# Graph attention with a planned order: five weight buffers in place of four, single buffers for the projections' pieces

## The chip, the core and the metric

The kernel runs on one core of a Trainium2 chip. A core has five engines with a queue each: TensorE (PE) multiplies matrices into PSUM, VectorE (DVE) and ScalarE (ACT) work elementwise on PSUM and SBUF, GpSimd (POOL) elementwise on SBUF, and SyncE (SP) issues transfers here. Each engine takes its instructions in the order of the program and waits on semaphores for what other engines owe it. The metric is the device time in microseconds (us) of one execution. Before the change three runs gave 6959.61 to 6975.31 us, with a median of 6971.53.

## What is computed

Two layers over a graph with N = 2708 nodes and D = 128 features. The second is small (two products of the 2708 x 2708 adjacency with a 2708 x 128 matrix). Nearly all the time is the attention of the first, which is unusual: after the projection, q, k and v are reshaped to (128, N, 8), so that there are 128 attentions, each over all N nodes with 8 channels, and all share one dense bias.

```python
q = (x @ Wq.T).reshape(d, n, h)          # d = 128, n = 2708, h = 8
k = (x @ Wk.T).reshape(d, n, h)
v = (x @ Wv.T).reshape(d, n, h)
a = jnp.einsum('dnh,dmh->dnm', q, k) * scale
a = a + adj + adj
a = jax.nn.softmax(a, axis=2)
out = jnp.einsum('dnm,dmh->dnh', a, v)
out = out.reshape(n, h * d) @ Wo.T
```

x is then normalised as layernorm(x + out), and the second layer follows. That makes 128 x 2708 x 2708, or 939 million, exponentials in float32.

## The kernel before

**Tiling.** The 128 attentions go in 32 groups of four (GB = 4), one per 32-row strip of TensorE. The queries of a group go in six blocks of 452 columns (QB; the last has 448). The 2708 keys are cut in 22 chunks: 21 of 128 and a short one of 20 (number NU = 21), whose four attentions share one tile. The scores lie transposed: keys on the partitions, queries along the row. The softmax takes no maximum away. The sum of the exps is had by a column of ones beside the values, so v has nine columns (VW).

**Steps and pieces.** The tiles (chunk, attention) of a block are shared out by `plan` over nine steps. A step has two to four *pieces* of two tiles each, 29 in a block, and one chunk called *two* of which three attentions' scores are taken another way. There are 32 x 6 x 9 = 1728 steps and 54 in a group. For a piece, TensorE writes two score tiles side by side into the PSUM tile s (`score`, L415, or L412 for the short chunk), and VectorE adds the adjacency to both and writes them into the step's tile e (`add_near`, L422). For the three tiles of *two*, TensorE writes scores into p, a PSUM tile with three banks. They are taken beside the pieces' own scores, on row strips that these leave free where possible. ScalarE takes the exp of p into w (L515) and GpSimd multiplies it by exp of twice the adjacency (L516, tile ecol), which stands for the addition. After a step's last piece ScalarE takes the exp of e in place (L518).

**Products.** When all four tiles of a chunk have their exps, `add_up` (L440; L437 for a block's first chunk, L432 for the short one) multiplies them with the values and adds into the single PSUM tile acc, one product per chunk, 22 in a block. A product of float32 shows as two instructions, so a chunk is eight of them. After a block's last product `hand_on` has VectorE copy acc to SBUF (L446) and SP store it in four transfers (L448).

**Buffers.** [...]s two tiles of two banks, p one of three, acc one. In SBUF, e has four buffers of 8 x 452 floats a partition (pool *weights*), w four (*products*), the adjacency comes in *cols* (9), *twos* (3) and *ecols* (7) and is issued eight tiles ahead by `load_adj`. The pool *proj* has two buffers each for four small tiles: xc (the chunk of x), wc (half of a weight matrix), pa (the projected half) and pr (that half rounded to the shorter float that the scores are multiplied in, and the remainder).

**Projections amid the attention.** Only two chunks of x are projected at the start. The rest, 120 halves, is projected in between, before piece 0 of the steps in `amid`: nine in group 0, six steps apart, then four in each group at its steps 2, 10, 18 and 26, until group 28. `project` has TensorE multiply wc into an s tile (L343), VectorE scale it into pa (L345), and leaves a list of *jobs*: for keys and queries two by GpSimd (L356, L357) and a store by SP (L352), for values the store alone (L347). One job is done per step, behind the score of its first piece (piece 1's position, L476). `load_half` for the next half is called at once, at the place of the projection.

**The order.** Nothing is left to a scheduler: instructions are issued as `interleave` yields them. It walks through a table of costs and decides whether TensorE goes on with a piece, a product or a projection. The argument `bufs` says how many e buffers it reckons with: a piece of step n is not to be had before the products with the tiles of step n - bufs stand in the order. It never yields a product before its exps are due by its costs. SP's queue follows the same program: the loads of a step at its piece 0, with eight transfers for the next block's queries at step 3 of a block (`load_q`, L287) ahead of that step's adjacency, and the stores of sums where `hand_on` comes.

Of the kernel before, what the change touches and what calls it, by code (L numbers as in the profile page):

```python
# [142 lines left out]
def graph_attention_gcn(ctx: ExitStack, tc: tile.TileContext, x, xT, adj, adjT, adjP, adjS,  # L143
# [20 lines left out]
    NU = NM - 1  # L164
# [24 lines left out]
    with ExitStack() as s:  # L189
# [28 lines left out]
        for m in range(NU):  # L218
            if m not in TWO_EXP:
                pairs += [[(m, 0), (m, 1)], [(m, 2), (m, 3)]]  # L220
            elif left_over.index(m) % 2:
# [4 lines left out]
        plan = [(pairs[cuts[i] : cuts[i + 1]], m, [j for j in range(GB) if j != left_out[m]])  # L226
                for i, m in enumerate(TWO_EXP)]
# [4 lines left out]
        steps = [(g, b, i) for g in range(NG) for b in range(len(QBS)) for i in range(len(plan))]  # L232
# [43 lines left out]
        def spread_values(g, j):  # L276
            to = vals[g % 2].rearrange("p c (j e) -> p j c e", e=VW)
            v = values[g][:, j, :].rearrange("p (c e) -> p c e", e=H)
            nc.gpsimd.tensor_copy(to[:, j, :, :H], v)
            nc.gpsimd.tensor_copy(v_first[g % 2][:, ds(32 * j, H)], v[:, first_chunk, :])  # L280

        def load_q(g, b):
            n0, nw = QBS[b]
            q = queries[g, b] = qpool.tile([P, QB], F32R, tag="q", name="q")
            for j in range(GB):
                for i in range(2):
                    nc.sync.dma_start(q[ds(32 * j + 2 * H * i, 2 * H), :nw].bitcast(F32),  # L287
                                      qs[:, ds((GB * g + j) * N + n0, nw)])
# [14 lines left out]
                nc.sync.dma_start(t[:, :nw], adjP[ds(m * P, P), ds(n0, nw)])  # L303

        ahead = 8
        epool = s.enter_context(tc.tile_pool(name="weights", bufs=4))
        ppool = s.enter_context(tc.tile_pool(name="products", bufs=4))
        opool = s.enter_context(tc.tile_pool(name="sums", bufs=2))
        proj = s.enter_context(tc.tile_pool(name="proj", bufs=2))
        ps = s.enter_context(tc.tile_pool(name="ps_s", bufs=2, space=PSUM))  # L310
        pq = s.enter_context(tc.tile_pool(name="ps_q", bufs=1, space=PSUM))
        pa = s.enter_context(tc.tile_pool(name="ps_a", bufs=1, space=PSUM))
# [15 lines left out]
        def load_half(n):  # L328
            c, i, h = halves[n]
            i0, mi = MC[c]  # L330
            if i == h == 0:
                given[c] = proj.tile([P, P], F32, tag="xc", name="xc")
                nc.sync.dma_start(given[c][:, :mi], xT[:, ds(i0, mi)])
            given[c, i, h] = proj.tile([P, NB], F32, tag="wc", name="wc")
            nc.sync.dma_start(given[c, i, h], projections[i][0][:, ts(h, NB)])

        def project(n):

            c, i, h = halves[n]
            i0, mi = MC[c]  # L340
            dst = projections[i][1]
            pp = ps.tile([P, 2, NB], F32, tag="s", name="s")
            nc.tensor.matmul(pp[:mi, 0, :], given[c][:, :mi], given.pop((c, i, h)), start=True, stop=True)  # L343
            a = proj.tile([P, NB], F32, tag="pa", name="pa")[:mi]
            nc.vector.tensor_scalar_mul(a, pp[:mi, 0], half_scale if i == 1 else 1.0)  # L345
            if i == 2:
                return [lambda: nc.sync.dma_start(dst.rearrange("(i g) e -> i (g e)", g=P)[ds(i0, mi), ts(h, NB)], a)]  # L347
            o = proj.tile([P, 2, NB], F32R, tag="pr", name="pr")[:mi]

            def store():  # L350
                for l in range(2):
                    nc.sync.dma_start(dst.rearrange("r (i g) -> i r g", g=P)[ds(i0, mi), ds(H * l + 4 * h, 4)],  # L352
                                      o[:, l].bitcast(F32).rearrange("p (e g) -> p e g", g=P))


            return [lambda: nc.gpsimd.tensor_copy(o[:, 0], a),  # L356
                    lambda: nc.gpsimd.tensor_sub(o[:, 1], a, o[:, 0].bitcast(F32)), store]  # L357
# [66 lines left out]
        def add_up(g, b, m, tiles):  # L424
            nw = QBS[b][1]
            _, _, v, vz = groups[g]
            if m == first_chunk:
                acc[g, b] = pa.tile([P, NB], F32, tag="acc", name="acc")
            a = acc[g, b]
            if m == NU:  # L430
                e, t = tiles[0]
                nc.tensor.matmul(a[:, :nw], vz, e[:, t, :nw], start=False, stop=False)  # L432
                return
            for j in range(GB):
                e, t = tiles[j]
                if m == first_chunk:
                    nc.tensor.matmul(a[ds(32 * j, 32), :nw], v_first[g % 2][:, ds(32 * j, 32)], e[:, t, :nw],  # L437
                                     start=True, stop=False)
                else:
                    nc.tensor.matmul(a[ds(32 * j, VW), :nw], v[:, m, ds(VW * j, VW)], e[:, t, :nw],  # L440
                                     start=False, stop=(m == last_chunk))

        def hand_on(g, b):
            n0, nw = QBS[b]
            o = opool.tile([P, QB], F32, tag="o", name="o")
            nc.vector.tensor_copy(o[:, :nw], acc.pop((g, b))[:, :nw])  # L446
            for j in range(GB):
                nc.sync.dma_start(os_[:, ds((GB * g + j) * N + n0, nw)], o[ds(32 * j, H + 1), :nw])  # L448
# [3 lines left out]
        amid = list(range(2, 54, 6)) + [54 * g + t for g in range(1, NG) for t in (2, 10, 18, 26)]  # L452
        amid = amid[: len(halves)]
        for g in range(1, NG):
            c = (min(NG, g + 2) * GB * N - 1) // (P * P)
            assert c < FIRST or amid[halves.index((c, 2, 1))] + 8 < 54 * g
        jobs = []
        loaded = ahead
        for what, n, c, beside in interleave(plan, len(steps) // len(plan), NU, amid):
            if what == "amid":  # L460
                at = amid.index(n)
                jobs += project(at)
                if at + 1 < len(halves):
                    load_half(at + 1)
                continue
            if what == "add_up":
                g, b = divmod(n, len(QBS))
                add_up(g, b, c, where.pop((g, b, c)))
                continue
            if what == "hand_on":  # L470
                hand_on(*divmod(n, len(QBS)))
                continue
            g, b, i = steps[n]
            pieces, two, _ = plan[i]
            nw = QBS[b][1]
            if c == 1 and jobs:  # L476
                jobs.pop(0)()
            if c == 0:
                nq = (g, b + 1) if b + 1 < len(QBS) else (g + 1, 0)
                if i == 3 and nq[0] < NG:  # L480
                    load_q(*nq)

                if g + 1 < NG:
                    t = b * len(plan) + i
                    if t < 32 and t % 2 == 0:
                        load_keys(g + 1, t // 2)
                    elif t < 32 and t % 8 == 7:
                        load_values(g + 1, t // 8)
                    elif 33 <= t < 50 and t % 2:
                        order_keys(g + 1, (t - 33) // 2)  # L490
                    elif t >= 50:
                        spread_values(g + 1, t - 50)
                last = max(loads.index((g, b, x), max(0, loaded - 40)) for x in [chunks_of(p) for p in pieces] + [-1 - two])
                while loaded < min(len(loads), last + 1 + ahead):
                    load_adj(loaded)
                    loaded += 1
                e = epool.tile([P, 8, QB], F32, tag="e", name="e")
                sp = pq.tile([P, 3, NB], F32, tag="p", name="p")
                w = ppool.tile([P, 3, QB], F32, tag="w", name="w")
                if g == 0:  # L500
                    first_exp(b, two)
                at = k = 0
            st = ps.tile([P, 2, NB], F32, tag="s", name="s")
            for r, (m, j) in enumerate(pieces[c]):
                score(st[:, r], g, b, m, j)
                where.setdefault((g, b, m), {})[j] = e, at + r
            for j in beside:
                score(sp[:, k], g, b, two, j)
                where.setdefault((g, b, two), {})[j] = w, k
                k += 1  # L510
            add_near(e, st, g, b, pieces[c], at)
            at += 2
            if c == len(pieces) - 1:
                look_at_near(g, b, two)
                nc.scalar.activation(w[:, :, :nw], sp[:, :, :nw], AF.Exp, scale=2.0)  # L515
                nc.gpsimd.tensor_mul(w[:, :, :nw], w[:, :, :nw],  # L516
                                     exp_cols[g, b, two][:, :nw].unsqueeze(1).to_broadcast([P, 3, nw]))
                nc.scalar.activation(e[:, :at, :nw], e[:, :at, :nw], AF.Exp, scale=2.0)  # L518
# [315 lines left out]
```

## Time and profile before

| | |
|---|---|
| timed runs, median (lowest to highest) | 6971.53 us (6959.61 to 6975.31) |
| profiled execution, its own time | 6986.59 us |
| its span | 6984.8 us |
| instructions in it | 137327 |
| mean TensorE clock granted, of full speed | 0.99 |
| moved by DMA | 1674.16 MB, mean 240 GB/s |
| first / last w exp (L515) starts at | 45.8 us / 6638.7 us |

The profile is one execution taken by the hardware. Busy time is the time in which an engine had an instruction running; matmuls are pipelined and their ends are modelled, so a busy TensorE is not one at its peak. "PEld" is its loading of weights, which lies beside the products. A group of instructions is told by its line in the kernel, engine, operation and tile. A wait is told by who waited (engine and line), who released it, the total of the idle time, how often and the longest. In the order of time, a line has the start and the duration in us, the engine, the line, the instruction, how many were merged into the line, and in brackets the idle time before it with what ended it. Stretches give, behind their length, the busy time of PE, PEld, DVE, ACT and POOL with the number of instructions, then the clock granted to TensorE, the share of DMA and GB/s.

The mean of one add on VectorE is 1091 ns, of one w exp 1340 ns, of one e exp 2677 ns (one for a whole step), of one multiply on GpSimd 3101 ns.

### The profile page before, as it was taken

The numbers are of one execution on the slowest core, as the hardware profiler recorded it, in microseconds if no ns is written. First come the engines' busy times: TensorE is split into PE (matmuls) and PEld (weight loads), VectorE is DVE, ScalarE is ACT, GpSimd is POOL, SyncE is SP. The second block draws the span as 40 slices with busy tenths as digits, with TensorE's granted clock in tenths as the row PEclk, the third lists the DMA queues.
The fourth block names the chain that finished last, engine by engine and source line by source line (L and its number), as shares of the span: only waits on it lengthen the run. The fifth ranks groups of instructions, "written<-read, shape, count | busy, mean of one in ns | idle before, by whom it ended". The sixth has DMA issues, their size and how long they took to land.

```text
span 6984.8 us, 137327 instructions
## 1 busy us (share of the span) xinstructions
PE 6734.9 (96%) x50426; PEld 2008.4 (29%) x50426; DVE 6129.9 (88%) x6307; ACT 6518.0 (93%) x3605; POOL 5761.0 (82%) x2546
## 2 busy tenths in 40 slices
PE   7999999999999999999999999999999999999979
PEld 2222222222222222222222222222222222222254
DVE  6899999999899999998998999999989999999941
ACT  7999999999999999999999999999999999999920
POOL 6888888888888888888888988889888888888800
PEclk8999999999999999999999999999999999999999
DMA  8877877777788777877777788877777877777667
GB/s 270 263 243 245 244 240 239 229 236 237 239 243 247 242 239 242 252 239 242 239 237 231 243 256 246 249 236 240 234 235 242 247 243 235 235 228 233 218 200 229
DMA packets 1143258, 1674.16 MB, mean 240 GB/s; under 512 B 148922, under 2 KB 1090366, under 8 KB 1138478
## 3 DMA queue, kind: packets, MB, share of 16 engines
q1 hardware_dynamic: 1142574, 1665.29, 77.5%
q8 instruction: 399, 6.54, 0.4%
q14 instruction: 285, 2.33, 0.1%
HBM read 1582.90 MB, written 81.80 MB: 238 GB/s over the span
## 4 chain that ended last, share of the span: by engine, by line
PE 48%; DMA 15%; DVE 12%; ACT 9%; issue 7%; SPq 5%; POOL 4%; DVEq 0%; ACTq 0%; POOLq 0%
PE acc L440 22%; PE s L415 16%; DVE e L422 10%; DMA col<-in_adjP 8%; ACT e L518 5%; POOL w L516 4%; ACT w L515 4%; PE acc L661 3%; DMA two<-in_adjP 2%; SPq L287 2%; PE acc L432 2%; PE p L415 2%; DMA ecol<-ne 2%; PE acc L437 1%; PE s L343 1%
## 5 line engine op out<-in xcount | busy, mean ns | idle before, releaser
L516 POOL TENSOR_TENSOR w<-w,ecol 128x1356 f32<-128x1356 f32 (+1 forms) x1728 | 5347.8, 3101 | 840.5 <-ACT w L515 740.9
L422 DVE TENSOR_TENSOR e<-s,col 128x904 f32<-128x904 f32 (+1 forms) x4608 | 4830.5, 1091 | 347.7 <-PE s L415 175.4
L518 ACT ACTIVATE e<-e 128x2712 f32<-128x2712 f32 (+5 forms) x1728 | 4625.7, 2677 | 33.5 <-DVE e L422 31.9
L440 PE MATMUL acc<-e,vals 128*9 128x452 f32 x20352 | 3591.7, 548 | 0.4 <-ACT e L518 0.2
L415 PE MATMUL s<-q,k 32*128 32x452 f32 x10944 | 2465.0, 465 | 175.3 <-DVE e L422 113.0
L515 ACT ACTIVATE w<-p 128x1356 f32<-128x1356 f32 (+1 forms) x1728 | 2316.0, 1340 | 98.7 <-PE p L415 84.1
L415 PEld LDWEIGHTS s<-q,k 32*128 32x128 f32 x10944 | 1016.3, 182 | 3414.6 <-DVE e L422 2974.0
L440 PE MATMUL acc<-w,vals 128*9 128x452 f32 x10368 | 1631.1, 547 | 0.0
L415 PE MATMUL p<-q,k 32*128 32x452 f32 (+1 forms) x5184 | 1334.6, 443 | 5.0 <-ACT w L515 4.4
L422 DVE TENSOR_TENSOR e<-s,two 128x904 f32<-128x904 f32 (+1 forms) x960 | 1047.8, 1091 | 173.7 <-PE s L415 92.9
L440 PEld LDWEIGHTS acc<-e,vals 128*9 128x9 f32 x20352 | 443.0, 88 | 782.1 <-issue 778.5
L415 PEld LDWEIGHTS p<-q,k 32*128 32x128 f32 x5184 | 546.1, 183 | 43.3 <-ACT w L515 29.5
L440 PEld LDWEIGHTS acc<-w,vals 128*9 128x9 f32 x10368 | 206.7, 88 | 221.9 <-issue 186.4
L262 POOL CAST k<-k_raw 128x336 fp32r<-128x336 f32 x251 | 222.3, 886 | 34.7 <-DMA q<-qs 34.7
L437 PE MATMUL acc<-e,v_first 128*32 128x452 f32 (+1 forms) x1536 | 187.5, 560 | 13.2 <-DVE o L446 3.6
L432 PE MATMUL acc<-e,v_short 128*128 128x452 f32 (+1 forms) x384 | 196.7, 594 | 0.0
L343 PE MATMUL s<-wc,xc 128*128 128x512 f32 (+1 forms) x240 | 133.8, 639 | 0.7 <-DVE e L422 0.4
L345 DVE TENSOR_SCALAR pa<-s 128x512 f32<-128x512 f32 (+1 forms) x120 | 82.8, 690 | 52.5 <-PE s L343 51.8
L446 DVE COPY o<-acc 128x452 f32<-128x452 f32 x192 | 118.4, 617 | 6.5 <-PE acc L440 6.5
L661 PE MATMUL acc<-col,xw 128*128 128x512 f32 (+2 forms) x264 | 106.0, 551 | 0.0
L661 PE MATMUL acc<-col,hw 128*128 128x512 f32 (+2 forms) x264 | 104.1, 545 | 0.0
L555 ACT ACTIVATE sd<-mv,eps 128x1 f32<-128x1 f32 (+1 forms) x22 | 5.9, 291 | 104.7 <-DVE mv L549 104.7
(84 smaller groups left out, 1067.2 us busy)
## 6 DMA issues: line engine op xcount, KB each, us to landing
col<-in_adjP SPq DMA_DIRECT2D x1965, 226.0 KB
two<-in_adjP SPq DMA_DIRECT2D x1440, 226.0 KB
ecol<-ne SPq DMA_DIRECT2D x1395, 226.0 KB
col<-in_adjP SPq DMA_DIRECT2D x393, 224.0 KB
two<-in_adjP SPq DMA_DIRECT2D x288, 224.0 KB
ecol<-ne SPq DMA_DIRECT2D x279, 224.0 KB
col<-in_adjT SPq DMA_DIRECT2D x210, 256.0 KB
k_raw<-ks SPq DMA_DIRECT2D x512, 84.6 KB
```

What stands on the lines that cost most here:

```text
L262: copy(k[:, :, ts(i, n)], t[:, ts(i, n * NU)].rearrange("p (q c) -> p c q", c=NU))
L287: nc.sync.dma_start(q[ds(32 * j + 2 * H * i, 2 * H), :nw].bitcast(F32), qs[:, ds((GB * g + j) * N + n0, nw)])
L343: nc.tensor.matmul(pp[:mi, 0, :], given[c][:, :mi], given.pop((c, i, h)), start=True, stop=True)
L415: nc.tensor.matmul(to[:, :nw], k[r, m, :], q[r], start=True, stop=True)
L422: nc.vector.tensor_add(e[:, ds(at, 2), :nw], st[:, :, :nw], a)
L432: nc.tensor.matmul(a[:, :nw], vz, e[:, t, :nw], start=False, stop=False)
L437: nc.tensor.matmul(a[ds(32 * j, 32), :nw], v_first[g % 2][:, ds(32 * j, 32)], e[:, t, :nw], start=True, stop=False)
L440: nc.tensor.matmul(a[ds(32 * j, VW), :nw], v[:, m, ds(VW * j, VW)], e[:, t, :nw], start=False, stop=(m == last_chunk))
L515: nc.scalar.activation(w[:, :, :nw], sp[:, :, :nw], AF.Exp, scale=2.0)
L516: nc.gpsimd.tensor_mul(w[:, :, :nw], w[:, :, :nw], exp_cols[g, b, two][:, :nw].unsqueeze(1).to_broadcast([P, 3, nw]))
L518: nc.scalar.activation(e[:, :at, :nw], e[:, :at, :nw], AF.Exp, scale=2.0)
L661: nc.tensor.matmul(acc[:, :nw], src[:mw, m, :], t[:mw, :nw], start=(m == 0), stop=(last is None and m == NM - 1))
```

## The change

The pool of e tiles gets a fifth buffer and `interleave` is called with `bufs=5`. The pool *proj* goes from two buffers to one for each of its four tiles. And the load of the next half is no longer issued at the projection: it becomes the last of the jobs, so it comes up three steps after the projection for keys and queries and one step after for values.

```diff
         ahead = 8
-        epool = s.enter_context(tc.tile_pool(name="weights", bufs=4))
+        epool = s.enter_context(tc.tile_pool(name="weights", bufs=5))
         ppool = s.enter_context(tc.tile_pool(name="products", bufs=4))
         opool = s.enter_context(tc.tile_pool(name="sums", bufs=2))
-        proj = s.enter_context(tc.tile_pool(name="proj", bufs=2))
+        proj = s.enter_context(tc.tile_pool(name="proj", bufs=1))
...
-        for what, n, c, beside in interleave(plan, len(steps) // len(plan), NU, amid):
+        for what, n, c, beside in interleave(plan, len(steps) // len(plan), NU, amid, bufs=5):
             if what == "amid":
                 at = amid.index(n)
                 jobs += project(at)
                 if at + 1 < len(halves):
-                    load_half(at + 1)
+                    jobs.append(lambda n=at + 1: load_half(n))
                 continue
```

An e tile takes 8 x 452 x 4 = 14464 bytes of a partition; the four tiles of *proj* together take 512 + 2048 + 2048 + 4096 = 8704 bytes, so the change adds 5760 bytes to a partition. The w tiles (*products*) stay at four and PSUM stays as it is.

Through `bufs`, the whole order of TensorE's instructions changes, and with it the place of `hand_on`: in the old order it comes behind piece 1 of a block's step 2 or just before the next, in the new order at step 3, which is behind the call of `load_q` in the program. The number of instructions of every kind stays the same.

## The prediction

> **What bounds the kernel now.** I read the shares of busy time first, then busy time by stretch, then the waits, then the order of instructions where a stretch loses time. Columns of a wait: total us, number of times, longest. One group is 54 steps; a step has one w exp and one e exp on ScalarE (L515, L518).
>
> ```profile
> PE 6734.9 (96%) x50426; PEld 2008.4 (29%) x50426; DVE 6129.9 (88%) x6307; ACT 6518.0 (93%) x3605; POOL 5761.0 (82%) x2546
> ```
>
> By share TensorE leads. By stretch it does not. These rows are busy times in three stretches cut at the start of a w exp: groups 8, 13 and 30.
>
> ```profile
> 1743.58:1954.33 210.75, 201.52 (x1542) 57.20 (x1538) 186.65 (x185) 201.66 (x109) 180.83 (x81) 0.98 0.78 237
> 2760.84:2963.55 202.71, 199.37 (x1542) 57.13 (x1538) 186.55 (x185) 200.91 (x110) 179.07 (x79) 1.00 0.81 245
> 6249.84:6450.00 200.16, 197.03 (x1533) 57.14 (x1531) 184.01 (x181) 200.16 (x109) 175.76 (x75) 1.00 0.75 233
> ```
>
> The fourth busy time is ScalarE's. In group 30, which has no projections, it is busy for 200.16 of 200.16 us: that is the floor of a group. Group 13, a quiet one with four projections, takes 202.71; group 8 takes 210.75, with the clock at 0.98. The starts of L515 in order of time give groups 1 to 28 together 5759.9 us; 28 floors of 200.2 are 5605.6. So **154 us** are lost where ScalarE starves, some 4 more in group 0, nothing after group 28. Who starves it:
>
> ```profile
> DVE e L422 <- PE s L415: 268.3, 654, 2.6
> ...
> ACT w L515 <- PE p L415: 84.1, 133, 3.3
> ```
>
> So TensorE is late for VectorE far more often than ScalarE stands still; only the second costs time. Two kinds of place carry the loss. The first is a projection, here group 13's at its step 18, seen on VectorE and then ScalarE (start, duration):
>
> ```profile
> 2826.26 0.69 DVE L345 TENSOR_SCALAR pa<-s 128x512 f32<-128x512 f32 x1 [0.42 <-PE s L343]
> ```
> ```profile
> 2831.36 3.22 ACT L518 ACTIVATE e<-e 128x3616 f32<-128x3616 f32 x1 [0.78 <-DVE e L422]
> ```
>
> VectorE idles 0.42 us for the projection's product, spends 0.69 on it, and five adds later ScalarE has nothing to exponentiate for 0.78 us. Such quiet groups (10, 13, 19, 22: 202.7 to 203.2) lose 2.6 us or so each: 28 x 2.6 = **73 us**. The rest, 154 - 73 = **81 us**, falls on groups of 204 to 211 us, mostly six steps into a block. Here is why, in SP's queue and on VectorE in group 8:
>
> ```profile
> 1813.74 2.44 SPq L448 DMA_DIRECT2D os<-o  x4
> 1816.47 5.45 SPq L287 DMA_DIRECT2D q<-qs  x8
> 1821.96 0.42 SPq L299 DMA_DIRECT2D ecol<-ne  x1
> 1822.43 0.43 SPq L296 DMA_DIRECT2D two<-in_adjS  x1
> ```
> ```profile
> 1827.90 1.10 DVE L422 TENSOR_TENSOR e<-s,two 128x904 f32<-128x904 f32 x1 [4.52 <-DMA two<-in_adjP]
> ```
> ```profile
> 1822.00:1832.00 10.00, 5.84 (x32) 1.56 (x27) 4.50 (x5) 7.60 (x5) 5.82 (x3) 0.72 0.92 263
> ```
>
> SP stores the sums and loads the next queries back to back, 8 us; the adjacency tile behind them lands 4.5 us late; TensorE idles, and its clock falls to 0.72 in those ten us.
>
> **The change, part by part.** *Order of products.* The order was worked out so that piece 0 of step n stands behind all products of step n-4; now n-5. Written out for both values, before 53% of the products stand three steps behind their last exp's step and the rest two steps; after, 31% stand four behind, 64% three. Between comparable pieces one or two products (0.88 us each, 2827.77 to 2828.65 in TensorE's timeline) move behind scores, so scores reach VectorE 0.9 to 1.8 us earlier after a projection. That is as much as a projection takes away (0.42 + 0.69). TensorE can pay it back, though barely: by its starts a block is 22 products of 0.88, 30 score pairs of 0.40 and six pairs of row groups met twice, 1.1 more, together 32.5 us; six blocks and four projections of 0.95 are 198.8, under ScalarE's 200.2. Against part one's 73 us: bounds 0 and 73. I take three quarters, **-55**, nearer the full one because the delays are about one product long; late next is the single p tile (the scores for the w exp wait until the last w exp has read it), which stays. A rule speaks against this: the Trainium skill, "TensorEngine Tiling", section PSUM Bottleneck, has tiling speed up TensorE but not the emptying of PSUM, which may become the bound; an SBUF buffer would then bring 0 and the sum stays 6985. The row says VectorE, which empties s, is busy 186.55 of 202.71 us, and it waits for TensorE 268 us in all; I follow the row.
>
> The new order also has 308 products directly behind another for 230, each 0.76 for 0.88 us (2833.74 to 2834.50 in the timeline): 78 x 0.12 = 9 us; and 939 pieces whose p scores share a row group for 1094, each 0.60 for 0.41 us (2831.61 to 2832.21 against 2827.36 to 2827.77): 155 x 0.19 = 29 us. Both lie beside ScalarE's work and are counted as nothing, but raise TensorE's room from 1.4 us a group to 2.6.
>
> *What else moves with it: hand-on.* The copy of the sums follows the last product, so it moves from piece 1 or 2 of a block's step 2 to piece 0 or 1 of step 3. Its four stores in SP's queue thereby pass behind the eight query loads and the adjacency loads issued at step 3 (three tiles, four DMAs). SP waits for that copy 983.2 us in all (176 times, up to 9.7); the query loads fill this wait instead of following it. At one such place late in the run SP issues nothing between 6240.31 and 6248.40, then four stores (1.39 us), eight queries (3.56 us) and only then a tile. After the change a tile follows the stores at once, 3.6 to 5.5 us earlier; the late tile was 4.5 us late. The skill's "DMA: Bandwidth & Descriptors", section Issuing engines are not separate DMA queues, holds the sequencer's time to issue for usually small beside the DMA; by it this move is worth 0. Here eight queries of 28.2 KB take 5.45 us to issue, and at the mean 240 GB/s their 226 KB take 0.94 us to move. The row decides: of 81 us, bounds 0 and 81, I take 60%, **-49**. The copy itself is between the same neighbours on VectorE and the first product of the next block still has two pieces before it: nothing.
>
> *Single buffers for projections.* xc, wc, pa and pr get one buffer; the load of the next half becomes a job, issued three steps after the projection (one for values) in place of with it, behind that step's adjacency and query loads, before the hand-on's stores where they meet. Each half adds one or two DMAs to another place in SP's queue (0.33 us each). Steps take 3.7 to 4.3 us and projections lie 6 or 8 steps apart, so the load has three steps left in group 0 and five later, 13 us and more. From DMAs issued and bytes moved I work out 3 to 4 us to landing. The product's buffer is free three steps before. pa is read by GpSimd's two copies (1.29 us for the second) two steps into the half, pr is stored by SP the step after, and both have three steps or more until rewritten. Bounds 0 and 120 halves x 1 us; I take **0**, hidden behind three or more steps of exps. Behind a late weight TensorE would hold scores, and with them all.
>
> *A new wait.* The w tiles remain four. The product that reads w of step n-4 now stands behind piece 0 of step n in 1136 steps, which costs nothing while it precedes the last piece; in 38 steps (mostly step 31 of a group) it stands behind it, and w's exp of step n waits for it. Behind that exp stand e's exp on ScalarE, GpSimd's multiply and the next p scores. A product is 0.88 us and about 0.2 until seen: 0 to 38 x 1.1 = 41 us. There ScalarE has little lead (0.2 us idle at step 31 in quiet groups), so I take a third, **+14**.
>
> Sum: -55 - 49 + 0 + 14 = -90. The profiled execution took 6986.6 (span 6984.8), so 6897; the three timed runs have a median of 6971.5, 15 below it, so **6880** as a median (6971.5 - 90, rounded).
>
> **Rivals.** *Full:* both losses go and ScalarE never starves before the end. For it: groups 29 to 31 run so with the same PSUM. Against it: clock drops. 6971.5 - 158 + 14 = 6828; 110 us or more gained is this case. *PSUM holds:* lead is set by one p and two s tiles, buffered products only wait elsewhere. For: TensorE waits for VectorE to free s (113 us). Against: 654 waits the other way. Only the queries' move pays, half of it: 6971.5 - 25 = 6946, down to no change. *Slower:* w is the bottleneck, four w tiles under an order for five. Place: L515 waiting for L440, in any of the 1136 steps where TensorE is late, ScalarE idling directly. Each wait costs up to a product and its signal, 1.1 us; from 104/1.1 = 95 waits, three or four a group, it decides; at six a group, 168 x 1.1 = 185, it gives 6971.5 - 104 + 185 = 7052. For: ScalarE is the bound. Against: the order has only 38 behind the last score. *It does not do what it says:* the order could hold nothing back because exps come late anyway; then 6971. Against: the products' places written out do shift.
>
> **How the numbers follow.** Forecast (40 to 110 gained) 0.52; full 0.20; PSUM or no effect 0.17, of which 0.10 gains more than 14 us; slower 0.11. A change within 0.2% (14 us) cannot be told from none. Faster 0.82, same 0.07, slower 0.11. The range leaves out the slower case and the outer part of full: 6830 to 6955.
>
> **What would show it.** Right: idle of L515 for p below 40 us; VectorE's idle for two and col (29.6 and 13.7) near a third; SP's wait for o well under 983; clock near 1.00 six steps into blocks; groups with projections at 201 to 203. Wrong: L515 or L518 waiting for L440; PE waiting for wc; groups still at 205 with the same gaps behind projections.

## The result and the profile after

The changed kernel takes 6904.0 us (median of four runs, 6901.14 to 6905.56); beside it the kernel before took 6965.57. The ratio is 0.991, with a 95% interval from 0.9893 to 0.9928: 62 us faster, where 90 were forecast. The two profiled executions lie further apart, 6986.59 and 6904.39 us, for a reason that matters below.

Busy time by stretch of the changed kernel, for groups 2, 8, 13 and 30, each cut within 0.4 us of its first w exp (columns as before: length, PE, PEld, DVE, ACT, POOL, clock, DMA, GB/s):

```profile
490.09:698.38 208.29, 198.84 (x1542) 55.76 (x1538) 191.66 (x197) 202.51 (x109) 181.09 (x81) 0.98 0.79 238
1721.82:1923.64 201.82, 197.61 (x1546) 55.98 (x1538) 186.22 (x185) 200.47 (x109) 180.69 (x81) 1.00 0.82 247
2730.48:2932.17 201.69, 197.47 (x1546) 55.95 (x1538) 186.02 (x185) 200.42 (x109) 179.18 (x79) 1.00 0.82 245
6158.94:6359.15 200.21, 193.45 (x1537) 57.43 (x1538) 182.46 (x181) 200.21 (x109) 175.80 (x75) 1.00 0.77 233
```

Four things are to be seen. Group 8, which took 210.75 us with a clock of 0.98, now takes 201.82 at 1.00. Group 13, quiet before at 202.71, gains 1.0 us and no more. Group 30 has the same floor as before, 200.21. From group 9 to group 28 all groups take 201.2 to 202.1 us; before, the same ones took 202.3 to 210.3. Groups 1 to 7 do less well: they still take 202.7 to 208.3 us, group 2 the most, and hold 33 of the 66 us by which groups 1 to 28 together still lie above the floor.

The waits that answer to those shown before, of the whole run, first VectorE's and ScalarE's, then SP's queue:

```profile
DVE e L422 <- PE s L415: 257.9, 568, 2.3
...
ACT w L515 <- PE p L415: 28.5, 45, 5.2
...
DVE e L422 <- DMA two<-in_adjP: 3.1, 7, 0.9
...
DVE e L422 <- DMA col<-in_adjP: 2.0, 7, 0.6
...
ACT w L515 <- PE acc L440: 0.4, 2, 0.2
```
```profile
SPq L448 <- DVE o L446: 439.9, 109, 6.7
```

ScalarE's wait for p falls from 84.1 to 28.5 us. VectorE's waits for adjacency tiles, 29.6 and 13.7 before, are 3.1 and 2.0. SP's wait for the copied sums falls from 983.2 to 439.9. VectorE's wait for TensorE's scores hardly moves, so the new order did not relieve VectorE in general. And w does not wait for old products: 0.4 us.

In SP's queue, the place in a block where SP went from the stores over the queries to the adjacency now looks like this (in group 13):

```profile
2800.28 5.82 SPq L287 DMA_DIRECT2D q<-qs  x8
2806.20 0.37 SPq L299 DMA_DIRECT2D ecol<-ne  x1
2806.67 0.38 SPq L296 DMA_DIRECT2D two<-in_adjS  x1
...
2807.57 0.42 SPq L303 DMA_DIRECT2D col<-in_adjP  x1
2808.30 1.38 SPq L448 DMA_DIRECT2D os<-o  x4
```

The queries still take 5.82 us to issue, but they and the adjacency of step 3 go out before SP comes to the copied sums.

### The profile page after: what moved, and what is told of

It reads as the page before. It is cut to its first block, busy times and chain, and to the rows that moved or that the text cites. A ratio compares the mean times of both kernels' runs of the same rounds, so it can differ in the third digit from the quotient of the medians.

```text
span 6902.6 us, 137500 instructions
## 1 busy us (share of the span) xinstructions
PE 6641.2 (96%) x50426; PEld 1983.7 (29%) x50426; DVE 6112.2 (89%) x6307; ACT 6501.8 (94%) x3605; POOL 5761.7 (83%) x2546
## 4 chain that ended last, share of the span: by engine, by line
PE 54%; DMA 13%; DVE 12%; POOL 8%; issue 6%; ACT 4%; SPq 3%; DVEq 0%; POOLq 0%; ACTq 0%
PE acc L440 27%; PE s L415 18%; DVE e L422 11%; POOL w L516 7%; DMA col<-in_adjP 4%; PE acc L661 3%; ACT w L515 2%; DMA k_raw<-ks 2%; PE p L415 2%; ACT e L518 2%; PE acc L437 2%; DMA two<-in_adjP 2%; DMA ecol<-ne 1%; PE s L343 1%; DMA q<-qs 1%
## 5 line engine op out<-in xcount | busy, mean ns | idle before, releaser
L518 ACT ACTIVATE e<-e 128x2712 f32<-128x2712 f32 (+5 forms) x1728 | 4747.6, 2747 | 17.4 <-DVE e L422 14.8
L440 PE MATMUL acc<-e,vals 128*9 128x452 f32 x20352 | 3553.2, 545 | 0.1
L415 PE MATMUL s<-q,k 32*128 32x452 f32 x10944 | 2501.3, 462 | 183.4 <-DVE e L422 117.7
L515 ACT ACTIVATE w<-p 128x1356 f32<-128x1356 f32 (+1 forms) x1728 | 2439.2, 1412 | 47.1 <-PE p L415 28.5
L415 PE MATMUL p<-q,k 32*128 32x452 f32 (+1 forms) x5184 | 1400.5, 446 | 18.7 <-ACT w L515 18.4
L415 PEld LDWEIGHTS p<-q,k 32*128 32x128 f32 x5184 | 575.5, 182 | 63.9 <-ACT w L515 53.6
```

What stands on the lines that cost most here:

```text
L415: nc.tensor.matmul(to[:, :nw], k[r, m, :], q[r], start=True, stop=True)
```

## The experiments

Each was timed in five rounds beside the kernel before on the same chip; its median there was between 6957.5 and 6965.6, so the ratios are the safer comparison.

### The order or the buffer

The changed kernel with the old order (five buffers, single projection buffers and late load kept):

```diff
-        for what, n, c, beside in interleave(plan, len(steps) // len(plan), NU, amid, bufs=5):
+        for what, n, c, beside in interleave(plan, len(steps) // len(plan), NU, amid, bufs=4):
```

> The changed kernel with TensorE's order worked out for four e buffers again (the five buffers, the single projection buffers and the later load of the half stay). Theory A (the order is what counts, a buffer alone buys nothing, and the projections' edits cost nothing): no change against the kernel before, 6966 us within 10. Rival (the fifth buffer itself lets VectorE run ahead): near 6904, as the changed kernel. If the projections' single buffers cost something that the order hides: slower than 6966 by over 14 us.

Measured: 6988.5 us, ratio 1.0029 (1.0017 to 1.0041). A buffer that the order doesn't use shows no gain here, as theory A had it; but its "no change" was missed too. What is left of the change, without the order, costs 20 to 25 us. So the projections' edits are not free in the old order.

### Only the place of the load

The kernel before, with the load of the next half made a job and nothing else:

```diff
-                    load_half(at + 1)
+                    jobs.append(lambda n=at + 1: load_half(n))
```

> The kernel before with only the load of the next half made a job; two projection buffers, four weight buffers and the old order stay. The changed kernel with the old order was 25 us slower than the kernel before. If the load's new place, in or just behind the stores and queries of SP's queue, is the reason: 6985 to 6990. If the single buffers are the reason: no change, 6963 within 8.

Measured: 6980.2 us, ratio 1.0023 (1.0017 to 1.003), 16 us slower. The load's place is most of the cost just seen; with intervals that overlap, nothing can be said of the single buffers beside it. VectorE's idle for two and col rose from 43.3 to 58.5 us. That the 256 KB come into the crowded part of SP's queue fits this; it was not tried by itself.

### SP's queue without the new order: early queries

The kernel before, queries one step earlier:

```diff
-                if i == 3 and nq[0] < NG:
+                if i == 2 and nq[0] < NG:
                     load_q(*nq)
```

> The kernel before with one edit: the eight query loads are issued at a block's step 2 in place of step 3, so they stand ahead of the stores of sums in SP's queue, which the change brings about as a side effect. Theory A (the gain comes half from products that stand later on TensorE, half from SP's queue): about 30 us faster, 6936. Rival B (SP's queue does it all): 6904 to 6910. Rival C (the order of products does it all): no change, 6966 within 10.

Measured: 6920.2 us, ratio 0.9937 (0.9924 to 0.9951), 43 us faster. One step's move of eight small transfers gives two thirds of what the change gives. Its stretches for groups 8 and 13:

```profile
1713.64:1916.46 202.82, 199.39 (x1546) 57.02 (x1538) 186.71 (x185) 200.88 (x110) 180.78 (x81) 1.00 0.80 245
2727.44:2930.19 202.75, 199.38 (x1546) 57.11 (x1538) 186.58 (x185) 200.90 (x110) 179.20 (x79) 1.00 0.80 244
```

Group 8 is now as quiet as group 13, and group 13 is what it was before (202.71). VectorE's idle for two and col falls from 43.3 to 16.1 us, and the stretches at half clock between 290 and 5900 us from 11 to one. So the late tile and the halved clock behind it were one loss and the projections another, and this edit takes the first alone.

### SP's queue without the new order: stores behind queries and adjacency

The kernel before, with the stores of the sums put off until SP has issued the queries and the adjacency of step 3, which is where the changed kernel has them:

```diff
+            def store():
-            for j in range(GB):
-                nc.sync.dma_start(os_[:, ds((GB * g + j) * N + n0, nw)], o[ds(32 * j, H + 1), :nw])
+                for j in range(GB):
+                    nc.sync.dma_start(os_[:, ds((GB * g + j) * N + n0, nw)], o[ds(32 * j, H + 1), :nw])
+            sums.append(store)
...
                     load_adj(loaded)
                     loaded += 1
+                if i == 3:
+                    while sums:
+                        sums.pop(0)()
```

> The kernel before with SP's queue alone in the changed kernel's order: the stores of the sums are issued behind the queries and the adjacency of a block's step 3; VectorE's copy, TensorE's order, four weight buffers and two projection buffers stay. Theory S: the late tiles go, and the quiet groups' 202.7 us holds for all groups as in the kernel with early queries, 6915 to 6920, and TensorE's new order brings the remaining 20 to 28 us down to the 6894 that the changed kernel takes with two projection buffers. Rival: the adjacency ahead of the stores brings more than the early queries did, down to 6900, and the new order next to nothing.

Measured: 6916.3 us, ratio 0.9936 (0.9923 to 0.995), the same as with early queries. VectorE's copy of the sums keeps its earlier place here, so SP waits for it even less than in the changed kernel (278.7 against 439.9 us). Under the old order SP's part is therefore worth about 0.0064, or 44 us, and can be had without touching TensorE's order.

### The queries put back in the changed kernel

```diff
-                if i == 3 and nq[0] < NG:
+                if i == 4 and nq[0] < NG:
                     load_q(*nq)
```

> The changed kernel with the query loads issued at a block's step 4, so they follow the stores of sums directly again, as before the change. Theory A: about 30 us slower than the changed kernel, 6934. Rival B: the gain is gone, 6955 to 6966. Rival C: as the changed kernel, 6904 within 8. VectorE's idle for adjacency tiles (5 us in the changed kernel, 43 before) should rise to 30 or more by A and B.

Measured: 6900.3 us, ratio 0.9907 (0.9892 to 0.9922): no loss, and both A and B are missed. By itself this looked as if SP's queue did not matter under the new order. But the edit only put the queries behind the stores; the adjacency of step 3 still stood ahead of both.

### All of SP's old order in the changed kernel

So the adjacency of step 3 went behind the hand-on as well:

```diff
             if what == "hand_on":
                 hand_on(*divmod(n, len(QBS)))
+                handed.add(n)
+                while late:
+                    late.pop(0)()
                 continue
...
-                if i == 3 and nq[0] < NG:
-                    load_q(*nq)
...
-                while loaded < min(len(loads), last + 1 + ahead):
-                    load_adj(loaded)
-                    loaded += 1
...
+                def feed(last=last, i=i, nq=nq):
+                    at_load = state["loaded"]
+                    if i == 3 and nq[0] < NG:
+                        load_q(*nq)
+                    while at_load < min(len(loads), last + 1 + ahead):
+                        load_adj(at_load)
+                        at_load += 1
+                    state["loaded"] = at_load
+                if i == 3 and n > 9 and n // 9 - 1 not in handed:
+                    late.append(feed)
+                else:
+                    feed()
```

> The changed kernel with the queries and the adjacency of a block's step 3 issued behind the hand-on, so SP's queue has the old order (stores of sums, queries, adjacency of step 3) under TensorE's new order. Theory S (what the change cured is SP's queue: late adjacency tiles): about 40 us slower than the changed kernel's 6900, so 6940, with VectorE's idle for adjacency tiles back above 25 us and the clock below 1.00 six steps into blocks. Rival P (products a step later give TensorE and VectorE the slack to stand a late tile): 6900 to 6908.

Measured: 7185.2 us, ratio 1.0335 (1.0309 to 1.0361): 281 us slower than the changed kernel, seven times the expected loss. Waits on VectorE, then in SP's queue:

```profile
DVE e L422 <- DMA two<-in_adjP: 219.2, 167, 3.5
...
DVE e L422 <- DMA col<-in_adjP: 44.8, 64, 2.1
```
```profile
SPq L448 <- DVE o L446: 1169.4, 181, 11.8
```

This refutes the rival that later products make late tiles harmless. It is also more than the old state: in the new order the hand-on stands later in the block, so adjacency behind it goes out later too. Counted in steps by ScalarE's w exps, the first adjacency tile behind the queries is issued 4.16 steps into a block in the median, against 3.75 in the kernel before. The expected 40 us forgot that.

Together the runs bound what has to pass ahead of the stores. In the old order the queries alone were enough (0.9937, with the adjacency of step 3 still behind the stores). In the new order the adjacency of step 3 alone was enough (0.9907, with the queries behind). With both behind, the new order loses all its gain and more. The queries alone in the new order were not tried.

### The fifth w buffer

```diff
-        ppool = s.enter_context(tc.tile_pool(name="products", bufs=4))
+        ppool = s.enter_context(tc.tile_pool(name="products", bufs=5))
```

> The changed kernel with five w buffers in place of four. The prediction put 14 us on exps of p that wait for a product with the old w: by that 6890. Rival: that wait is not there (the trace of the changed kernel has 0.4 us of it), then 6904 within 8.

Measured: 6900.9 us, ratio 0.9911 (0.9897 to 0.9924), as the changed kernel. The new wait on w is not there.

### Two projection buffers and the early load under the new order

```diff
-        proj = s.enter_context(tc.tile_pool(name="proj", bufs=1))
+        proj = s.enter_context(tc.tile_pool(name="proj", bufs=2))
...
-                    jobs.append(lambda n=at + 1: load_half(n))
+                    load_half(at + 1)
```

> The changed kernel with two projection buffers and the load of the next half at the projection again, as before the change; five weight buffers and the new order stay. The changed kernel's group 0 takes 238.9 us against 231.6 in the kernel before with early queries, with TensorE idle for wc for 5.8 us. If the late load costs that: about 7 us faster than 6900, near 6893. If group 0's time has another cause, or the load lands in the way of adjacency tiles: 6900 within 4.

Measured: 6894.0 us, ratio 0.9899 (0.9885 to 0.9913), as expected for the first case. The changed kernel's waits in group 0 (45 to 290 us) have these rows, of which this kernel has none for wc:

```profile
PE s L343 <- DMA wc<-in_WvT: 3.4, 1, 3.4
...
PE s L343 <- DMA wc<-in_WkT: 2.2, 1, 2.2
```

Group 0 takes 235.3 us in place of 238.9. The difference of the ratios, 0.0011 or 8 us, is within their intervals, and group 0 accounts for 3.5 us of it in these two traces; so the waits for wc are shown, and a cost of 8 us is not. The two edits were undone together, so which of them delays the weights is open. Five e buffers and two projection buffers fit together, so the single buffers were not needed.

### What a projection still costs, and where

The changed kernel's group 13 still loses 0.86 us at its third projection, the one at step 18. TensorE, then VectorE and ScalarE:

```profile
2793.83 1.12 PE L343 MATMUL s<-wc,xc 128*128 128x512 f32 x2
2794.89 0.95 PE L440 MATMUL acc<-e,vals 128*9 128x452 f32 x8
2795.76 0.52 PE L415 MATMUL s<-q,k 32*128 32x452 f32 x4
...
2798.80 0.47 PE L415 MATMUL p<-q,k 32*128 32x452 f32 x2
```
```profile
2796.36 1.10 DVE L422 TENSOR_TENSOR e<-s,col 128x904 f32<-128x904 f32 x1 [0.67 <-PE s L415]
```
```profile
2799.40 1.31 ACT L515 ACTIVATE w<-p 128x1356 f32<-128x1356 f32 x1 [0.86 <-POOL w L516]
```

A product stands between the projection and the next scores; VectorE idles 0.67 us; the last scores into p end at 2799.27 (2798.80 + 0.47), and the exp follows at 2799.40. The bracket names GpSimd, but TensorE's scores end last. The only other idle time of ScalarE in group 13 is 0.41 us at step 5, behind the projection at step 2. Behind the projections at steps 10 and 26 there is none, so the projections were moved within their blocks:

```diff
-        amid = list(range(2, 54, 6)) + [54 * g + t for g in range(1, NG) for t in (2, 10, 18, 26)]
+        amid = list(range(2, 54, 6)) + [54 * g + t for g in range(1, NG) for t in (1, 10, 19, 28)]
```

First with five buffers (two projection buffers, load at the projection):

> The changed kernel with two projection buffers, the load at the projection, and the projections of groups 1 to 28 at steps 1, 10, 19 and 28 in place of 2, 10, 18 and 26. What is left in the changed kernel's groups is 0.5 us behind the projection at step 2 and 1 us at the one at step 18, and nothing at steps 10 and 26. If the phase within a block is what costs: groups of about 200.5, 1.2 us x 28 = 34 us faster than 6894, so 6860. If the loss is a projection's own work, wherever it stands: 6894 within 8.

Measured: **6852.9 us, ratio 0.9848** (0.9835 to 0.9862), 105 us faster than the kernel before beside it and the fastest of all. Its stretches for groups 8, 13 and 20:

```profile
1705.46:1905.61 200.15, 196.59 (x1542) 56.70 (x1538) 185.62 (x186) 200.05 (x109) 180.56 (x81) 1.00 0.81 245
2706.20:2906.30 200.10, 196.46 (x1542) 56.98 (x1538) 185.23 (x185) 200.10 (x109) 179.03 (x79) 1.00 0.81 247
4107.19:4307.38 200.19, 196.58 (x1542) 56.94 (x1538) 185.33 (x185) 200.19 (x109) 180.79 (x81) 1.00 0.80 245
```

ScalarE works without a gap beside four projections: the floor of the groups without any. All of groups 8 to 28 take 200.0 to 200.2 us; groups 1 to 7 still take 201.4 to 209.3. Then the same places with four buffers, the old order rule and SP's new queue:

> The kernel before (four weight buffers, old order rule, two projection buffers) with SP's queue in the changed kernel's order and the projections of groups 1 to 28 at steps 1, 10, 19 and 28. The same projections under five buffers gave 6853. If the fifth buffer and its order are what lets the other engines absorb a projection: above 6880, groups with projections at 201.5 or more. If the projections' places alone decide: 6853 to 6870, groups at 200.2 to 200.6, and the fifth buffer is worth little once they stand well.

Measured: 6924.3 us, ratio 0.994 (0.9927 to 0.9954): nothing against 0.9936 without the move. So the places alone give nothing. With them, the fifth buffer and its order are worth 0.994 - 0.9848 = 0.0092, or 64 us; with the old places, as the next section works out, 26.

## Why the prediction came out as it did

**What bounds the kernel:** right. ScalarE's floor of 200.2 us a group stood in every trace, and the last but one experiment reached it in groups with projections. That TensorE has barely enough room (198.8 by its starts) also held: there it is busy 196.5 us of 200.1. Two readings of the trace were off without harm to the argument. The stretches given for groups 8 and 30 have the right length but start 9.4 and 8.0 us into their group; cut at its first w exp, ScalarE is busy 201.66 of 210.75 and 200.16 of 200.16 us, as stated. And four adds, not five, lie between the projection and ScalarE's idle 0.78 us.

**The late tile:** the mechanism was right: stores and queries together, the tile behind them, TensorE idle, the clock down. The prediction took 49 us; SP's queue alone brought 44 (0.0064). The rule that issuing is usually small beside the transfer (the Trainium skill, "DMA: Bandwidth & Descriptors", section Issuing engines are not separate DMA queues), by which this part would be 0, did not hold for these eight small loads: they took 5.45 us to issue, and moving them alone brought 43 us. The queries that it named were enough by themselves in the old order; which of the moved loads carries the gain in the changed kernel is not separated, as the adjacency was enough there too.

Not all of the 81 us put down to late tiles was theirs. With SP's queue set right and the old order, groups 1 to 7 still take 203.3 to 207.7 us, together 20 us above seven quiet groups of 202.7. What marks groups 0 to 7 is a reduction of the tile ecol on VectorE (L404), 108 times 0.61 us, the last at 1727 us. It is the likely cause, but no run leaves it out, so that is not shown. These groups hold half of what the changed kernel still loses, and all that is left once the projections are moved.

**The order of products:** the mechanism works, but this is the term that was mis-sized. Three quarters of 73 us were taken for it, -55; it measured 0.9936 - 0.9899 = 0.0037, or 26 us, from SP's queue alone to the order with it, and 1.0 of 2.6 us in a quiet group. The step that failed is the reason given for the three quarters, that a deferral as long as the delay covers it. The traces show where it did. With SP's queue set right and the old order, ScalarE idles in the mean of groups 8 to 28 for 0.42 us at step 5, 0.42 at step 14 and 0.77 at step 18; with the new order the idle time at step 14 is gone, and 0.40 at step 5 and 0.82 at step 18 stay as they were. So the deferral covered the projection at step 10, but not those at steps 2 and 18. With places that suit it, buffer and order are worth what was hoped for and a little more (64). The rule that the emptying of PSUM may become the bottleneck (the Trainium skill, "TensorEngine Tiling (Array Packing)", section PSUM Bottleneck), by which this part would be 0, does not bind here: the run with the moved projections keeps ScalarE busy for 200.10 of 200.10 us with PSUM unchanged.

**The projections' buffers at 0:** taken too low. Three steps of cover were reckoned, and TensorE waited for wc in group 0 all the same, 3.4 and 2.2 us, one of the signs of being wrong that the prediction lists. The group took 3.5 us longer than with the early load; by the ratios the cost is 8 us, within the intervals.

**The wait on w at +14:** not there (0.4 us in the trace, nothing with a fifth w buffer). The slower rival had its ground in this and goes with it. Its third rested on a misread step: in the trace of before ScalarE never idles at step 31 of groups 1 to 28; what it idles (0.19 us on average in groups 8 to 28) is at step 32.

**Sum:** -44 - 26 + 8 = -62, against -90. The three are differences of ratios along one chain of runs, from the kernel before to the changed one, so they add up to the measured gain by construction; another chain could split it otherwise. Against the prediction, the order fell 29 us short, the late tile 5, the projections' buffers 8, and the 14 for w, set against the gain, were not needed: 29 + 5 + 8 - 14 = 28. That the 14 hid half of the order's shortfall was luck. The base matters besides: the losses were read from a profiled execution that took 15 us more than the median then known and 21 more than the later one. In profiled executions the gain was 82 us, 63 of it from SP's part. Time and clock vary together: in 26 executions of the kernel before, made beside three of the runs, it took from 6951 us at a mean clock of 0.993 to 6981 at 0.989, while five with early queries lay within 7 us.

Of the rivals, "full" was not reached by this change, though the projections' move comes near it (105 us gained, where "full" began at 110); "PSUM holds" falls with that run. The cheaper products and p scores of the new order (9 and 29 us of TensorE) were not tried by themselves.

## What to carry to other kernels

When one buffer is added and an order reworked for it, write out what else moves in every queue: here two thirds of the gain came from four stores that a program's order let pass behind loads in SP's queue, and it could be had by one line without the buffer. A wait in a queue that only issues transfers need not cost anything until something urgent stands behind it (SP still waits 440 us for the copied sums in the changed kernel), so put what waits for late results behind what is needed soon. And slack from a buffer is worth most after the disturbances have been placed where it can be spent; try the two together before judging either.

## What had not been expected

Small shifts in one issuing queue span 285 us in this kernel (6900 with the queries alone behind the stores, 7185 with the adjacency behind them too), far more than all of TensorE's reordering: late tiles idle TensorE, and the mean granted clock falls from 0.993 to 0.977, which lengthens what follows. Between 290 and 5900 us the clock record of the trace of before has 11 windows at half clock, of 3.4 or 6.8 us, that of the changed kernel one, and that of the run at 7185 has 54. Six of the 11 begin beside one of the eight adjacency tiles for which VectorE waited more than 1.5 us. The idle stretches of TensorE at their start are short: at one window it lasts 4.1 us, and in the 8 us ahead of the other ten none is over 2.2 us.
